# Up-projections of the last layer's experts in four column groups of the array

## The chip, the cores and the metric

The kernel runs on one core of a Trainium2 chip. The metric is the device time of one execution in microseconds. Everything is computed in 32-bit floats. The engines are named as in the profile: PE is TensorE (PEld its weight loads), DVE is VectorE, ACT is ScalarE, POOL is GpSimd, SP issues most transfers.

## The reference, cut to what matters

The input x is 32 batches of 128 tokens with 128 features. Two layers follow each other, each with a residual. The change is in the second, L1:

```python
# L1_cond: two shared experts and eight routed ones, 4096 tokens of 128 features
for e in range(2):
    h = silu(x @ s_w1[e].T) * (x @ s_w3[e].T)      # 128 -> 256
    shared_out += h @ s_w2[e].T                    # 256 -> 128
for e in range(8):
    h = gelu(x @ r_w1[e].T)                        # 128 -> 128
    routed_out += h @ r_w2[e].T * gates_full[:, e] # top 2 of 8
out = (shared_out / 2 + routed_out) / 4
# L1_ffn: a low-rank feed-forward layer on that
P = out @ U1                                       # 128 -> 32
H = gelu(P @ V1 + b1)                              # 32 -> 512
x = x + (H @ U2) @ V2 + b2                         # 512 -> 32 -> 128
```

## The kernel before

Activations are kept with the 128 features on the partitions and the tokens in the free dimension, in 8 blocks of 512 tokens (`TB`). In L1 four blocks make a superblock (`SB = 4`), so there are two superblocks (`NS`). A matmul of one block streams 512 columns and fills one tile of 128 x 512 in PSUM; the pool for these tiles (`mm_tile`) has six buffers, and a second pool (`y_tile`) has two for sums.

The down-projections of the L1 experts are folded with U1 ahead of time (`fold_down`), so that each maps 128 hidden features to 32 outputs. `into` issues four matmuls of 32 columns, one for each block of a superblock: block j writes partitions 32j to 32j+31 of one PSUM tile, which selects column group j of the array. The sum over all experts stays in that tile, `low_p` (`p_ps` in the profile).

The up-projections use the full array. `sh_up` makes, for each of the four blocks, a gate and an up matmul (`g` at line 627, `u` at line 628 of the profile's numbering), then ACT's Silu and DVE's product (`glu`, lines 509 and 510) into `h`. `r_up` makes one matmul per block (`ur`, line 650), ACT's Gelu into `ar` (line 652) and DVE's product with the gate `rg` (line 653), which POOL spreads from one row to all partitions (`spread`, line 504, six buffers). The low-rank layer has its own units: `low_up` (`ul`, line 670) uses four row groups of the array, and its way down (`q_ps`) uses `into` again.

The order is a list of units: the shared ones ("s", 4 for each superblock), the routed ones ("r", 8 for each superblock), and the low-rank ones ("l"). `pipelined` issues the up-projection of unit i+1 ahead of the down-projection of unit i:

```python
units = [("s", sb, k) for sb in range(NS) for k in range(4)]
units += [("r", 0, e) for e in range(E1)]
units += [("r", 1, 0), ("r", 1, 1)]
units += [("l", 0, c) for c in range(NC - 1)]
units += [("r", 1, e) for e in range(2, E1)]
units += [("l", 0, NC - 1)]
units += [("l", 1, c) for c in range(NC)]
```

In between, `l1_scores` (matmuls `l_ps` in column groups, then transposes `l_b` on the full array), `route` and `gates_to_dram` (a transpose `rg_ps`) prepare the second superblock's gates. The framework puts the instructions of each engine in order by their place in the program and by when it expects their inputs, and sets the semaphores. Ahead of L1 lie the L0 layer's experts (up to about 190 us) and its feed-forward part (matmuls `g`, `u` at lines 522 and 523, `yf` at line 209), which ends at 852.3 us.

Of the kernel before, what the change touches and what calls it, by code (L numbers as in the profile page):

```python
# [43 lines left out]
SB = 4  # L44
# [47 lines left out]
def adaln_ffn(  # L92
# [3 lines left out]
    nc = tc.nc  # L96
# [9 lines left out]
    def mm_tile(name):  # L106
        return psum.tile([P, TB], F32, tag="mm", name=name, bufs=6)
# [393 lines left out]
    def spread(row, name):  # L501

        bc = work.tile([P, TB], F32, tag="bc", name=name, bufs=6)
        nc.gpsimd.partition_broadcast(bc, row)  # L504
        return bc

    def glu(ps_gate, ps_up, h, name):
        s = work.tile([P, TB], F32, tag="sg", name=name, bufs=4)
        nc.scalar.activation(s, ps_gate, AF.Silu)  # L509
        V.tensor_tensor(h, s, ps_up, ALU.mult)  # L510
# [76 lines left out]
    sws_t = wpool.tile([P, 2, 2, 2, P], F32, tag="w0", name="sws_t")  # L587
    sw2s_t = wpool.tile([P, 2, 2, P], F32, tag="w1", name="sw2s_t")
    rw1_t = wpool.tile([P, E1, P], F32, tag="w2", name="rw1_t")
# [6 lines left out]
    x1T = xT  # L596
# [19 lines left out]
    def into(y, w, h, first, last):  # L616

        for j in range(SB):
            nc.tensor.matmul(y[32 * j : 32 * (j + 1), :], lhsT=w, rhs=h[:, j, :], start=first, stop=last)  # L619

    def sh_up(sb, k):
        e, c = divmod(k, 2)
        h = work.tile([P, SB, TB], F32, tag="h", name=f"hs_{sb}_{k}", bufs=3)
        for j in range(SB):
            x = x1T[SB * sb + j]
            g, u = mm_tile(f"g1_{sb}_{k}_{j}"), mm_tile(f"u1_{sb}_{k}_{j}")
            nc.tensor.matmul(g, lhsT=sws_t[:, 0, e, c, :], rhs=x, start=True, stop=True)  # L627
            nc.tensor.matmul(u, lhsT=sws_t[:, 1, e, c, :], rhs=x, start=True, stop=True)  # L628
            glu(g, u, h[:, j, :], f"s1_{sb}_{k}_{j}")
        return h  # L630

# [12 lines left out]
    def r_up(sb, e):  # L644
        h = work.tile([P, SB, TB], F32, tag="h", name=f"hr_{sb}_{e}", bufs=3)
        g, k = divmod(e, 4)
        for j in range(SB):
            gate = spread(grows[sb][32 * k : 32 * k + 1, g, j * TB : (j + 1) * TB], f"rg_{sb}_{e}_{j}")
            ps = mm_tile(f"ur_{sb}_{e}_{j}")
            nc.tensor.matmul(ps, lhsT=rw1_t[:, e, :], rhs=x1T[SB * sb + j], start=True, stop=True)  # L650
            a = work.tile([P, TB], F32, tag="sg", name=f"ar_{sb}_{e}_{j}", bufs=4)
            nc.scalar.activation(a, ps, AF.Gelu)  # L652
            V.tensor_tensor(h[:, j, :], a, gate, ALU.mult)  # L653
        return h
# [24 lines left out]
    def low_out(sb):  # L679
        q = work.tile([P, TB], F32, tag="qT", name=f"qT{sb}", bufs=1)  # L680
        V.tensor_copy(q, held["q", sb])
        for j in range(SB):
# [6 lines left out]
            queue.dma_start(out=out[SB * sb + j], in_=t)  # L689

    STAGES = {"s": (sh_up, sh_down), "r": (r_up, r_down), "l": (low_up, low_down)}
    units = [("s", sb, k) for sb in range(NS) for k in range(4)]
    units += [("r", 0, e) for e in range(E1)]
# [112 lines left out]
```

## Time and profile before

| | |
|---|---|
| median of 3 runs | 1026.9 us (1026.76 to 1027.1) |
| the profiled execution's own time | 1027.21 us |
| its span, first to last instruction | 1025.4 us |
| mean granted TensorE clock | 0.998 |
| TensorE busy | 1010.3 us, 99% of the span, 2894 matmul records |
| shared and routed part of L1 | 852.3 to 1000.2 us |
| what follows (last low-rank units, output) | 1000.2 to 1025.4 us |

An fp32 matmul appears as two records and two weight loads. Matmuls overlap in the pipeline, so the busy time and the duration of a record are longer than what it adds; the distance between starts tells what a matmul costs. In a line of the timeline the first number is the start in us, the second the length of the stretch, "x8" the records merged into it; "128\*32" are the rows and columns of the array that a matmul uses. What stands in brackets is idle time ahead and what ended it.

### The profile page before, as it was taken

What the parts mean: (1) busy time and instruction counts of PE and PEld (TensorE: products, weight loads), DVE (VectorE), ACT (ScalarE), POOL (GpSimd) and SP (SyncE); (2) the same over time, 40 slices, a digit from 0 to 9 for tenths busy, and PEclk for the clock granted to TensorE, in tenths of its full rate; (3) what the DMA queues carried; (4) which work ended last, traced back from release to release, by engine and by line L of the source; (5) the groups of instructions that cost most, each with busy time, mean ns of one, the idle gap of its engine ahead of it and who ended that gap; (6) DMA issues with size and microseconds to landing.
All of it is one profiled execution on the core that took longest, in us unless ns stands there. A gap on an engine that the chain in (4) does not pass through costs nothing.

```text
span 1025.4 us, 8650 instructions
## 1 busy us (share of the span) xinstructions
PE 1010.3 (99%) x2894; PEld 484.4 (47%) x2894; DVE 457.3 (45%) x811; ACT 332.8 (32%) x575; POOL 143.9 (14%) x142
## 2 busy tenths in 40 slices
PE   7999999999999999999999999999999999999997
PEld 3378888444445444444444444444444444333332
DVE  4424443445433434343436444444433334547582
ACT  4445444423221222222223222222222223335754
POOL 0000000031111111111111111111111002008670
PEclk9999999999999999999999999999999999999999
DMA  9235555000000000000000000000000000000002
GB/s 316 94 125 165 176 169 167 25 2 1 3 2 0 1 0 2 0 1 1 1 0 1 0 3 2 0 1 0 1 0 1 0 1 3 1 5 1 1 1 82
DMA packets 18699, 34.66 MB, mean 34 GB/s; under 512 B 1680, under 2 KB 9872, under 8 KB 18640
## 3 DMA queue, kind: packets, MB, share of 16 engines
q1 hardware_dynamic: 17792, 32.61, 9.9%
q10 hardware_dynamic: 864, 1.52, 0.4%
q8 instruction: 22, 0.36, 0.1%
q14 instruction: 21, 0.17, 0.1%
HBM read 31.76 MB, written 2.36 MB: 33 GB/s over the span
## 4 chain that ended last, share of the span: by engine, by line
PE 98%; DVE 1%; DMA 0%; DVEq 0%; issue 0%; ACTq 0%
PE yf L209 21%; PE g L522 21%; PE u L523 21%; PE y L209 6%; PE u L203 6%; PE ur L650 6%; PE us L203 3%; PE g L627 3%; PE u L628 3%; PE p_ps L619 2%; PE ys L209 2%; PE ul L670 1%; PE q_ps L619 1%; DMA sw_t<-in_sw 0%; PE fold_ps L603 0%; PE o_ps L685 0%
## 5 line engine op out<-in xcount | busy, mean ns | idle before, releaser
L509 ACT ACTIVATE sf<-g 128x512 f32<-128x512 f32 x256 | 152.7, 597 | 495.4 <-PE g L522 494.3
L510 DVE TENSOR_TENSOR hf<-sf,u 128x512 f32<-128x512 f32 x256 | 175.8, 687 | 207.2 <-PE u L523 206.1
L522 PE MATMUL g<-c0all,wg_t 128*128 128x512 f32 x512 | 261.6, 592 | 0.0
L523 PE MATMUL u<-c0all,wu_t 128*128 128x512 f32 x512 | 261.4, 592 | 0.0
L209 PE MATMUL yf<-hf,wd_t 128*128 128x512 f32 x512 | 230.5, 592 | 0.0
L504 POOL PARTITION_BROADCAST fg<-fgT x64 | 77.8, 1228 | 720.2 <-DVE tf L536 516.5
L209 PEld LDWEIGHTS yf<-hf,wd_t 128*128 128x128 f32 x512 | 97.0, 190 | 123.0 <-issue 123.0
L523 PEld LDWEIGHTS u<-c0all,wu_t 128*128 128x128 f32 x512 | 97.3, 190 | 122.4 <-issue 120.5
L522 PEld LDWEIGHTS g<-c0all,wg_t 128*128 128x128 f32 x512 | 96.7, 190 | 120.5 <-issue 118.4
L536 DVE TENSOR_TENSOR tf<-yf,fg 128x512 f32<-128x512 f32 x64 | 44.2, 691 | 167.5 <-PE yf L209 162.0
L504 POOL PARTITION_BROADCAST rg<-grows x64 | 65.0, 1118 | 129.9 <-DVE hr L653 80.3
L204 ACT ACTIVATE h<-u,w 128x256 f32<-128x256 f32 x136 | 58.5, 474 | 62.1 <-PE u L203 62.1
L653 DVE TENSOR_TENSOR hr<-ar,rg 128x512 f32<-128x512 f32 x64 | 56.6, 911 | 24.4 <-ACT ar L652 22.9
L203 PE MATMUL u<-x,w 128*128 128x256 f32 x272 | 64.3, 379 | 0.0
L209 PE MATMUL y<-h,w 128*128 128x256 f32 x272 | 64.3, 379 | 0.0
L650 PE MATMUL ur<-xall,rw_t 128*128 128x512 f32 x128 | 59.2, 605 | 0.0
L203 PEld LDWEIGHTS u<-x,w 128*128 128x128 f32 x272 | 51.7, 190 | 7.9 <-issue 1.0
L209 PEld LDWEIGHTS y<-h,w 128*128 128x128 f32 x272 | 51.7, 190 | 7.5 <-issue 0.5
L652 ACT ACTIVATE ar<-ur 128x512 f32<-128x512 f32 x64 | 37.9, 598 | 32.8 <-PE ur L650 31.1
L537 DVE TENSOR_TENSOR xall<-xall,tf 128x512 f32<-128x512 f32 x64 | 45.4, 709 | 2.1
L650 PEld LDWEIGHTS ur<-xall,rw_t 128*128 128x128 f32 x128 | 23.0, 189 | 36.4 <-issue 25.2
L388 DVE SCALAR_TENSOR_TENSOR t<-y,w 128x256 f32<-128x256 f32 x34 | 16.5, 484 | 53.0 <-PE y L209 53.0
(168 smaller groups left out, 472.9 us busy)
## 6 DMA issues: line engine op xcount, KB each, us to landing
w<-in_experts SPq DMA_DIRECT2D x34, 578.5 KB
xall<-in_x SPq DMA_DIRECT2D x8, 256.0 KB
wg_t<-in_w_gate SPq DMA_DIRECT2D x8, 256.0 KB
wu_t<-in_w_up SPq DMA_DIRECT2D x8, 256.0 KB
wd_t<-in_w_down SPq DMA_DIRECT2D x8, 256.0 KB
rw_t<-in_r_w SPq DMA_DIRECT2D x2, 512.0 KB
out<-fin SPq DMA_DIRECT2D x4, 256.0 KB
out<-fin ACTq DMA_DIRECT2D x4, 256.0 KB
```

The costliest lines, as they stand in the source:

```text
L203: nc.tensor.matmul(ps[c], lhsT=w[:, c * P : (c + 1) * P], rhs=rhs, start=True, stop=True)
L204: nc.scalar.activation(h[:, c, :], ps[c], AF.Gelu_apprx_tanh, bias=bias[:, c : c + 1])
L209: nc.tensor.matmul(y[:, :n], lhsT=w[:, c, :], rhs=h[:, c, :n], start=(c == 0), stop=(c == NC - 1))
L504: nc.gpsimd.partition_broadcast(bc, row)
L509: nc.scalar.activation(s, ps_gate, AF.Silu)
L510: V.tensor_tensor(h, s, ps_up, ALU.mult)
L522: nc.tensor.matmul(g, lhsT=wg_t[:, e, cs], rhs=c0T[blk], start=True, stop=True)
L523: nc.tensor.matmul(u, lhsT=wu_t[:, e, cs], rhs=c0T[blk], start=True, stop=True)
L536: V.tensor_tensor(t, y, spread(fgates[blk][32 * k : 32 * k + 1, g, :], f"fg_{blk}_{e}"), ALU.mult)
L537: V.tensor_tensor(xT[blk], xT[blk], t, ALU.add)
L650: nc.tensor.matmul(ps, lhsT=rw1_t[:, e, :], rhs=x1T[SB * sb + j], start=True, stop=True)
L653: V.tensor_tensor(h[:, j, :], a, gate, ALU.mult)
```

## The change

A helper `from_x` issues an up-projection as four matmuls, each with 32 of the 128 weight columns and with the same x. Matmul j writes partitions 32j to 32j+31 of the same PSUM tile, that is, it uses column group j. `sh_up` and `r_up` call it in place of their full matmuls. What is computed, the tiles and the readers stay the same.

```diff
+    def from_x(ps, w, x):
+
+        for j in range(4):
+            own = slice(32 * j, 32 * (j + 1))
+            nc.tensor.matmul(ps[own, :], lhsT=w[:, own], rhs=x, start=True, stop=True)
+
     def sh_up(sb, k):
...
-            nc.tensor.matmul(g, lhsT=sws_t[:, 0, e, c, :], rhs=x, start=True, stop=True)
-            nc.tensor.matmul(u, lhsT=sws_t[:, 1, e, c, :], rhs=x, start=True, stop=True)
+            from_x(g, sws_t[:, 0, e, c, :], x)
+            from_x(u, sws_t[:, 1, e, c, :], x)
...
     def r_up(sb, e):
...
-            nc.tensor.matmul(ps, lhsT=rw1_t[:, e, :], rhs=x1T[SB * sb + j], start=True, stop=True)
+            from_x(ps, rw1_t[:, e, :], x1T[SB * sb + j])
```

## The prediction, made before the changed kernel ran

> **What bounds the kernel now.** I read the page's busy times first, then the chain of waits, then the timeline of the stretch that the change edits, and last the windows of the three parts of that stretch.
>
> ```profile
> PE 1010.3 (99%) x2894; PEld 484.4 (47%) x2894; DVE 457.3 (45%) x811; ACT 332.8 (32%) x575; POOL 143.9 (14%) x142
> ...
> PE 98%; DVE 1%; DMA 0%; DVEq 0%; issue 0%; ACTq 0%
> ```
>
> TensorE is busy for 99% of the span and carries 98% of the chain that ended last. What counts is how many matmul passes TensorE streams and what it loses between them. An fp32 matmul leaves two records (two passes). The shared up-projections show the price of a pass:
>
> ```profile
> 888.94 1.02 PE L627 MATMUL g<-xall,sws_t 128*128 128x512 f32 x2
> 889.80 1.02 PE L628 MATMUL u<-xall,sws_t 128*128 128x512 f32 x2
> 890.66 1.02 PE L627 MATMUL g<-xall,sws_t 128*128 128x512 f32 x2
> 891.51 1.02 PE L628 MATMUL u<-xall,sws_t 128*128 128x512 f32 x2
> 892.47 1.06 PE L619 MATMUL p_ps<-hs,fold 128*32 128x512 f32 x8
> 893.46 1.12 PE L627 MATMUL g<-xall,sws_t 128*128 128x512 f32 x2
> ```
>
> The reader is to read starts, not durations, since the records overlap. Full matmuls start 0.858 us apart (888.94 to 891.51 is three of them, 2.57), so a pass costs 0.429. The down-projection is one row of eight records: four matmuls of 32 columns, two passes each, and the next full matmul starts 0.99 after it. Four quarter-wide matmuls together thus cost little more than one full one. But the seams are not free: 891.51 to 892.47 is 0.96 where 0.858 would do, and 892.47 to 893.46 is 0.99. The routed stage repeats this, and shows the other engines:
>
> ```profile
> 922.33 3.70 PE L650 MATMUL ur<-xall,rw_t 128*128 128x512 f32 x8
> ...
> 925.96 1.07 PE L619 MATMUL p_ps<-hr,fold 128*32 128x512 f32 x8
> ...
> 926.96 3.70 PE L650 MATMUL ur<-xall,rw_t 128*128 128x512 f32 x8
> ...
> 929.73 4.11 POOL L504 PARTITION_BROADCAST rg<-grows  x4 [0.49 <-DVE hr L653]
> ...
> 931.58 0.30 PEld L650 LDWEIGHTS ur<-xall,rw_t 128*128 128x128 f32 x2 [0.84 <-ACT ar L652]
> ```
>
> A routed unit takes 4.63 us (922.33 to 926.96, and 4.627 as the mean to 936.21). It streams 8 passes up and 2 down: 10 x 0.4292 = 4.292. So 0.335 is lost per unit in going from the full array to four column groups and back. A shared unit takes 8.06 (884.41 to 892.47) for 18 passes, 7.725: again 0.335. By single starts, going into column groups loses 0.117 (0.094 before the first, 0.024 before the second pass, whose weights were not loaded ahead), going back 0.218. The two weight loads bunched at 931.58, "x2" in 0.30, are the back side of it: they could not be loaded ahead.
>
> What happens between two column-group sets, with no full matmul between:
>
> ```profile
> 866.16 1.07 PE L619 MATMUL p_ps<-hs,fold 128*32 128x512 f32 x8
> ...
> 867.04 1.04 PE L421 MATMUL l_ps<-xall,par 128*32 128x512 f32 x8
> ...
> 867.90 1.02 PE L619 MATMUL p_ps<-hs,fold 128*32 128x512 f32 x2
> ```
>
> 866.16, 867.04, 867.90: 0.88, then 0.86. Nothing is lost between sets of one shape, though weights, sources and targets all change.
>
> **The change part by part.** Each of 128 full matmuls (64 shared: 8 units x 4 blocks x gate and up; 64 routed: 16 x 4) becomes four of 32 columns, side by side, into the four partition quarters of the same tile.
>
> *Streaming.* A set of four streams 512 columns per group, twice, as the full matmul did: 0.858 by the rows above. Cost against before: zero, if four streams run at once. Here the four read one x, where the down-projection reads four slices; no row shows that. The streams start some 7 ns apart, so they are not on one address at one time. I take zero; the other end, two streams at a time, would be 128 x 0.86 = +110 us, and nothing in the trace points there.
>
> At this place the Trainium skill speaks against the change: "TensorE: Matmul & The Clock Gate", section Measured speedup vs the span model, gives four row groups 3.07 times and three column groups 2.38 times one matmul's rate, not 4 and 3. At 77% of the ideal a set would cost 0.858 / 0.77 = 1.11, and 128 sets +33 us. This case's row (0.88 and 0.86 per set of four) is 97 to 100%. I take the row: those figures look like ones for a lone set with its latency, but here sets follow one another.
>
> *Seams removed.* Counted along TensorE's order from 852.33 to 1000.20. Into column groups: 7 in the shared part, 10 up to 962.98, 6 after 970.90, together 23. Back to the full array: 5 in the shared part (that ahead of rg_ps stays), 9, then 1 at 970.90 and 5 after, together 20. New ones into column groups: 3, where the first shared up follows yf (852.33), and after the transposes l_b and rg_ps. Net 20 in and 20 back, 20 x 0.335 = 6.7 us. The seams of the low-rank units (ul in row groups) and of the transposes stay. All 20 lie on the chain, where TensorE never idles (the windows show it busy 65.40 of 65.40 and 82.50 of 82.50 us).
>
> *Instructions added.* 128 x 3 x 2 = 768 weight loads and as many matmul records. A set of four is 8 pairs of load and matmul in 0.858 us, one pair per 107 ns. Is that rate to be had for long? Bounds from the trace: at 63 to 150 us TensorE runs 405 pairs in 87 us with no gap, 215 ns a pair, but streaming sets that pace. fold_ps has 24 pairs 112 ns apart, set by their 128-column loads. Five tiny matmuls (gate_ps to t_ps, 10 pairs) take 31 ns a pair, and from 962.98 to 970.90 there are 56 pairs at 141 ns, every hole of which has a named waiter. All short ones can come from a filled queue, so the trace bounds the sustained cost of a pair only between 31 and 215 ns. The same page (Part 1, Wait — 56ns, not 53.3ns?) gives 62 ns of sequencer work per MATMUL if hardware decode is off: 8 x 62 = 0.50 per set, hidden under 0.858; if a load cost as much, 0.99 per set and not hidden. Its section Back-to-back issue gap gives 81 ns for a load-matmul pair in a stream: 0.65, hidden. I take zero, the nearest rows being the bursts, and keep the dear end as a rival. Instruction fetch: the page's 22 packets (0.36 MB) grow by about a quarter, with DMA at 1% in this stretch; the stage at 63 to 150 us uses up instructions at half the needed rate without a stall. Zero.
>
> *Waits.* Each set signals about 20 ns later (the last of four). ACT and DVE start later by that, TensorE does not. In the shared part ACT idles 1.12 us before each activation, so it follows; its idle time covers the 4% faster pace.
>
> *What is late next.* In the routed part a unit shrinks to 4.29. POOL needs 4.11 for its four broadcasts; DVE 3.5 for four products. Both slow each other when both are full:
>
> ```profile
> 974.20 10.91 DVE L653 TENSOR_TENSOR hr<-ar,rg 128x512 f32<-128x512 f32 x11 [9.30 <-ACT ar L652]
> ...
> 974.98 10.79 POOL L504 PARTITION_BROADCAST rg<-grows  x10 [8.75 <-DVE hr L653]
> ```
>
> That is 0.99 a product and 1.08 a broadcast, against 1.073 per block from TensorE. DVE keeps up; POOL is level with it, and starts six tiles ahead (six buffers). Cost zero, with little room. The tail from 1000.20 (25.2 us, paced by ACT, DVE and the output) only moves earlier.
>
> **Sum.** 0 (streaming) + 0 (issue) + 0 (waits) - 6.7 = -6.7 us. The profiled execution took 1027.2 (span 1025.4), so it would be 1020.5; it stands 0.3 above the median of the runs, 1026.9, and the median becomes 1020.2.
>
> **The rivals.**
>
> *Issue cannot keep four groups fed* (slower). Place: the 152 sets, 128 up and 24 down, between 852 and 1000. It decides above 107 ns for a pair of load and matmul; at 113 ns it eats the whole gain (152 x 8 x 5.5 ns = 6.7). With 62 ns for a load as for a matmul, 124 a pair, it is 152 x 0.133 = +20.2, less 6.7: 1040.4. For: no row shows a pair under 112 ns for longer than a queue may hold, and the routed and shared stages need it for 55 us and more. Against: the small bursts at 31 ns, and the 81 ns of the page. Chance 0.16.
>
> *POOL or DVE sets the pace of the routed part* (a smaller gain). The page's mean of a routed broadcast is 1118 ns: 4.47 per unit, 0.18 over 4.29, over 16 units 2.9 us, less the lead of six tiles that hides some. With waits handed back and forth it may be 4: 1021 to 1024. Chance 0.09. For: 0.49 of POOL's time per unit is a wait for DVE. Against: the saturated stretch at 974.20, where it ran 1.08.
>
> *The seams stay or come back in another form* (no change): for instance weights of a column group that are exposed at each set, 0.05 x 128 = 6.4. The l_ps row speaks against it. 1026.5 to 1027, chance 0.05.
>
> **How the numbers follow.** Full gain 0.70, 1020.2, within 1018.5 (a TensorE hole such as the 0.1 us ahead of l_b filled, one seam more or less) and 1021.5. Adding the second rival and the lower part of the third gives 8 in 10 up to 1025. The runs of this kernel lie within 0.03%, and about 0.2%, 2 us, is what a measurement can tell from no change. Faster by over 0.2%: 0.70 + 0.08 = 0.78; same: 0.05 + 0.01 = 0.06; slower: 0.16.
>
> **What would show it.** Right: the page counts 3662 matmul records; in the timeline the routed unit takes 4.29 and the shared one 7.73; up and down rows of 128*32 follow each other with no 0.52 between last starts; p_ps ends about 6.7 us earlier, near 993.5; the tail is unchanged. Issue bound: sets of four start 0.95 to 1.0 apart with no releaser named but "issue", evenly. POOL bound: TensorE gaps only in the routed part, ahead of p_ps, released by DVE hr, DVE waiting for rg. The prediction is wrong if four groups reading one x stream slower than 0.86 per set, or if the order of matmuls comes out differently and lets p_ps split the sets.

## The result, and the profile after

The changed kernel takes 1020.67 us (median of 6 runs, 1020.39 to 1021.55), the kernel before 1027.07 beside it: 6.4 us less, a ratio of 0.9938 with a 95% interval of 0.9926 to 0.9951. Forecast were 1020.2 us, 6.7 us less. The profiled execution took 1021.55 us, with a span of 1019.6.

The page of the kernel after, first the busy times, then the chain:

```profile
PE 1004.8 (99%) x3662; PEld 478.4 (47%) x3662; DVE 460.4 (45%) x811; ACT 332.6 (33%) x575; POOL 145.7 (14%) x142
...
PE 98%; DVE 1%; DMA 0%; DVEq 0%; issue 0%; ACTq 0%
```

TensorE has 768 records and as many weight loads more, is still busy for 99%, and still carries 98% of the chain. The time came out of TensorE itself. The timeline of TensorE in the shared part of the kernel after:

```profile
914.49 1.04 PE L625 MATMUL g<-xall,sws_t 128*32 128x512 f32 x8
915.35 1.04 PE L625 MATMUL u<-xall,sws_t 128*32 128x512 f32 x8
916.20 1.04 PE L619 MATMUL p_ps<-hs,fold 128*32 128x512 f32 x8
917.06 1.47 PE L625 MATMUL ur<-xall,rw_t 128*32 128x512 f32 x12
```

and in the routed part:

```profile
921.35 3.62 PE L625 MATMUL ur<-xall,rw_t 128*32 128x512 f32 x32
924.79 1.04 PE L619 MATMUL p_ps<-hr,fold 128*32 128x512 f32 x8
925.65 3.62 PE L625 MATMUL ur<-xall,rw_t 128*32 128x512 f32 x32
929.08 1.04 PE L619 MATMUL p_ps<-hr,fold 128*32 128x512 f32 x8
929.94 2.33 PE L625 MATMUL ur<-xall,rw_t 128*32 128x512 f32 x20
```

Every row starts a whole number of 0.858 us after the one ahead: 914.49, 915.35, 916.20, 917.06, and 921.35 to 924.79 is four of them. The 0.96 and 0.99 around the down-projection are gone. A routed unit takes 4.29 us (921.35, 925.65, 929.94) where it took 4.63.

All starts of the part, from the first shared matmul to the last down-projection, can be added up. Each full matmul of 512 columns, or set of four, is charged 0.858, a single quarter of a set a quarter of that, a transpose of 128 columns 0.107; what is left between starts is loss. The part of it that stands at a change of tile shape is what the prediction calls a seam:

| from the first shared matmul to the last p_ps | before | after |
|---|---|---|
| whole, us | 147.87 | 141.19 |
| streaming as charged, up to the last start, us | 137.49 | 137.49 |
| loss between shared, routed and down matmuls | 6.72 | 0.08 |
| loss around l_b and rg_ps | 1.07 | 1.41 |
| loss around ul and q_ps | 2.60 | 2.21 |

Streaming is a charge here and not a measurement: that it is the same says only that as many columns stream. That a set of four takes no longer than a full matmul is shown by the starts above, and by the 0.08 us that are left between sets. The loss fell from 10.39 to 3.70 us: 6.68 less, with the rounding.

### The profile page after: what moved, and what is told of

Its sections match the earlier page's. It is cut to its first block, busy times and chain, and to the rows that moved or that the text cites. A ratio compares the mean times of both kernels' runs of the same rounds, so it can differ in the third digit from the quotient of the medians.

```text
span 1019.6 us, 10200 instructions
## 1 busy us (share of the span) xinstructions
PE 1004.8 (99%) x3662; PEld 478.4 (47%) x3662; DVE 460.4 (45%) x811; ACT 332.6 (33%) x575; POOL 145.7 (14%) x142
## 4 chain that ended last, share of the span: by engine, by line
PE 98%; DVE 1%; DMA 0%; DVEq 0%; issue 0%; ACTq 0%
PE yf L209 22%; PE g L522 22%; PE u L523 22%; PE u L203 6%; PE y L209 6%; PE ur L625 5%; PE us L203 3%; PE g L625 3%; PE u L625 3%; PE ys L209 2%; PE p_ps L619 2%; PE ul L676 1%; PE q_ps L619 1%; DMA sw_t<-in_sw 0%; PE fold_ps L603 0%; PE o_ps L691 0%
## 5 line engine op out<-in xcount | busy, mean ns | idle before, releaser
L659 DVE TENSOR_TENSOR hr<-ar,rg 128x512 f32<-128x512 f32 x64 | 59.9, 981 | 15.9 <-ACT ar L658 15.4
L625 PE MATMUL ur<-xall,rw_t 128*32 128x512 f32 x512 | 58.4, 592 | 0.0
L625 PE MATMUL g<-xall,sws_t 128*32 128x512 f32 x256 | 42.0, 593 | 0.0
L625 PE MATMUL u<-xall,sws_t 128*32 128x512 f32 x256 | 42.0, 592 | 0.0
```

Source lines behind the costliest of these rows:

```text
L625: nc.tensor.matmul(ps[own, :], lhsT=w[:, own], rhs=x, start=True, stop=True)
```

## The experiments

Times of whole kernels carry some tenths from elsewhere in the program, so each verdict rests on two numbers: the timed runs, and the length of this part in the profile. The one repeat of that second number, the changed kernel run again beside e9, gave 141.20 after 141.19.

**One half of the change alone.** In e1 `r_up` keeps its full matmul (the edit below, against the changed kernel), in e2 `sh_up` does.

```diff
-            from_x(ps, rw1_t[:, e, :], x1T[SB * sb + j])
+            nc.tensor.matmul(ps, lhsT=rw1_t[:, e, :], rhs=x1T[SB * sb + j], start=True, stop=True)
```

Expected of e1:

> Only the shared up-projections are issued in column groups; the routed ones keep the full array. Theory (the gain is the seams removed, 0.117 us into column groups and 0.218 us back): of the shared part's seams 7 into column groups go and 3 new ones come, and 4 back go (the one ahead of the first routed unit stays): 4 x 0.117 + 4 x 0.218 = 1.3 us faster than before. Rival (four quarter-wide matmuls stream faster or slower than a full one, so the effect goes with the number of matmuls): half of the 6.4 us, 3.2, since 64 of the 128 matmuls are shared.

Expected of e2:

> Only the routed up-projections are issued in column groups. Theory (seams): 16 seams into column groups and 16 back go and none comes, 16 x 0.335 = 5.4 us faster than before. Rival (effect per matmul): 3.2 us, as for the shared half.

Measured: e1 1025.92 beside 1027.27 us, ratio 0.9986 (0.9979 to 0.9992), this part 146.44, so 1.43 shorter than before. e2 1022.14 beside 1027.27, ratio 0.9946 (0.9933 to 0.9960), this part 142.62, 5.25 shorter. The rows of TensorE show the seams that each keeps, first the routed ones of e1, then the shared ones of e2:

```profile
921.63 3.70 PE L656 MATMUL ur<-xall,rw_t 128*128 128x512 f32 x8
925.26 1.06 PE L619 MATMUL p_ps<-hr,fold 128*32 128x512 f32 x8
926.26 3.70 PE L656 MATMUL ur<-xall,rw_t 128*128 128x512 f32 x8
```

```profile
892.27 1.02 PE L634 MATMUL u<-xall,sws_t 128*128 128x512 f32 x2
893.22 1.07 PE L619 MATMUL p_ps<-hs,fold 128*32 128x512 f32 x8
894.21 1.13 PE L633 MATMUL g<-xall,sws_t 128*128 128x512 f32 x2
```

Both halves have 64 matmuls, yet one brings nearly four times the other. The effect goes with the number of seams, not of matmuls. 1.43 and 5.25 add up to 6.68. In e1, as in the changed kernel, the new seam of 0.09 between `yf` and the first shared matmul lies ahead of this part and is not in these numbers (last section).

**Fewer seams without column groups.** e3 takes the kernel before and issues two units at a time (its tile buffers change too, as the expectation says):

```diff
...
+    while at < len(units):
+        n = 1 if units[at][0] == "l" else 2
+        groups.append(units[at : at + n])
+        at += n
...
+    pipelined(groups, group_up, group_down)
```

> The kernel before, with full up-projections, but shared and routed units taken in pairs: two up-projections, then the two down-projections of the pair before. Four buffers for h in place of three, and two small tiles share others' buffers to make room. Theory (seams): about half of the seams go, 13 instead of 23 into column groups and 10 instead of 20 back, 10 x 0.335 = 3.3 us faster than before, some tenths more or less from the changed order around the low-rank units. Rival (the gain comes from column groups as such, their loads or their streaming): no change.

Measured: 1024.99 beside 1027.27 us, ratio 0.9980 (0.9972 to 0.9987); this part 145.90, so 1.97 shorter, where 3.3 was expected. The loss between shared, routed and down matmuls fell from 6.72 to 3.18, 3.54 less: the seams did go, with full matmuls only. The way into the low-rank units took 1.6 of it back. The timeline of e3, TensorE, shows the place:

```profile
959.43 2.76 PE L620 MATMUL p_ps<-hr,fold 128*32 128x512 f32 x18
962.93 1.14 PE L671 MATMUL ul<-pT,par 32*128 32x512 f32 x8 [0.73 <-DVE pT L662]
```

With both down-projections of a pair issued together, the low-rank up-projection comes straight behind the sum it reads, and waits for DVE's copy of it. In the kernel before a routed up-projection stood between.

**Is it the full array, or any change of shape?** e4 uses two groups of 64 columns:

```diff
-        for j in range(4):
-            own = slice(32 * j, 32 * (j + 1))
+        for j in range(2):
+            own = slice(64 * j, 64 * (j + 1))
```

> The changed kernel with two groups of 64 columns in place of four of 32. Theory that a seam is paid for any change of tile shape: the seams between 64 and 32 columns stay and some new ones come at the edges, so about the time of before (1026.5 to 1027.5). Rival, that a seam is paid only between the whole array and column groups: about the time of the changed kernel (1020 to 1021). Two groups of 64 should stream at the same 0.858 us per set.

Measured: 1026.76 beside 1027.27 us, ratio 0.9995 (0.9987 to 1.0004); this part 147.29, 0.58 shorter. The timed runs cannot tell it from no change. The timeline of e4, TensorE:

```profile
923.50 3.65 PE L625 MATMUL ur<-xall,rw_t 128*64 128x512 f32 x16
927.08 1.07 PE L619 MATMUL p_ps<-hr,fold 128*32 128x512 f32 x8
928.08 2.37 PE L625 MATMUL ur<-xall,rw_t 128*64 128x512 f32 x10
```

923.50 to 928.08 is 4.58: the unit still loses 0.29 of 0.335, and from the down-projection to the next matmul it is 1.00 as before. So two groups of 64 stream at full rate too, but a seam is paid between these two shapes as well. What the change needs is not smaller tiles but the same tiles as its neighbour.

The weight loads show what became cheaper, first the kernel before, then e4:

```profile
926.96 0.30 PEld L650 LDWEIGHTS ur<-xall,rw_t 128*128 128x128 f32 x2 [0.84 <-ACT ar L652]
927.49 0.19 PEld L650 LDWEIGHTS ur<-xall,rw_t 128*128 128x128 f32 x1 [0.24 <-issue]
```

```profile
928.07 0.20 PEld L625 LDWEIGHTS ur<-xall,rw_t 128*64 128x64 f32 x4 [0.84 <-ACT ar L658]
928.56 0.14 PEld L625 LDWEIGHTS ur<-xall,rw_t 128*64 128x64 f32 x2 [0.29 <-issue]
```

The third load of a unit (in e4, of each group) starts with its second pass. The second pass comes 0.53 us after the first in the kernel before and 0.48 in e4 (by the starts in ns), where 0.43 would do: the second load behind a seam, not made ahead, costs 0.10 with 128 columns and 0.05 with 64. The rest of the seam, 0.10 ahead of `p_ps` and 0.11 behind it in e4, is about what it was (0.09 and 0.11). What TensorE does in that time no run shows.

**How much issue is there to spare?** e5 and e6 cut each matmul along the tokens, into two and four:

```diff
+        n = TB // 4
+        for i in range(4):
+            t = slice(i * n, (i + 1) * n)
...
-            nc.tensor.matmul(ps[own, :], lhsT=w[:, own], rhs=x, start=True, stop=True)
+                nc.tensor.matmul(ps[own, t], lhsT=w[:, own], rhs=x[:, t], start=True, stop=True)
```

Expected of e5:

> The changed kernel with each matmul of the up-projections cut in two along the tokens (256 columns streamed instead of 512): twice as many pairs of weight load and matmul for the same streaming, one pair per 54 ns where the changed kernel needs one per 107. Theory (issue has room): the time of the changed kernel, 1020.7, up to 1.5 us more for the extra starts. Rival (issue is near its limit): with c ns a pair a set costs 16 c once that is over 858; at c = 62 it is 0.99 us and the kernel 128 x 0.134 = 17 us slower than the changed one.

Expected of e6:

> As the one with half rows, but cut in four (128 columns streamed): one pair per 27 ns. Here the limit should show: at 31 ns a pair (the burst of tiny matmuls ahead of the gates) a set of 32 pairs costs 0.99 us and the kernel is 17 us slower than the changed one; at 62 ns 1.98 us and 144 us slower; if nothing limits at 27 ns, within 3 us of the changed one. The time gives c.

Measured: e5 1021.14 us, this part 141.80; e6 1022.34 us, this part 143.02. Both stay close to the changed kernel: 0.61 and 1.83 us longer in this part, which is 4.8 ns for each of the 128 and 384 added sets (two passes each, so 2.4 ns a pass). The timeline of e6, TensorE:

```profile
921.53 3.68 PE L628 MATMUL ur<-xall,rw_t 128*32 128x128 f32 x128
925.03 1.04 PE L619 MATMUL p_ps<-hr,fold 128*32 128x512 f32 x8
```

128 pairs of load and matmul in 3.50 us (921.53 to 925.03) are 27 ns a pair. The changed kernel needs one per 107. Between units come the eight pairs of a down-projection at 107 ns, during which later pairs might be made ready; over a whole routed unit, 136 pairs in 4.35 us, it is 32 ns. That rate was held through the routed units without a limit showing. Whether 27 ns could be held without these breaks was not tried.

**Does POOL or DVE pace the routed part?** e7 spreads one gate row per unit:

```diff
-            gate = spread(grows[sb][32 * k : 32 * k + 1, g, j * TB : (j + 1) * TB], f"rg_{sb}_{e}_{j}")
+            if j == 0:
+                gate = spread(grows[sb][32 * k : 32 * k + 1, g, :TB], f"rg_{sb}_{e}")
```

> The changed kernel, with one gate row spread for each routed unit in place of four, used for all its blocks (the gates of three blocks in four are left out): POOL does a quarter of its work there and DVE is no longer slowed by it. Theory (TensorE alone paces the routed part after the change): the time of the changed kernel within 0.5 us. Rival (POOL or DVE paces it, or holds the last sum back): 1 to 4 us faster.

Measured: 1020.27 us, this part 141.10 (0.09 shorter), what follows it 24.88 in place of 25.19. That 0.31 came behind the issue of the last output transfers (1014.78 us, in e7 1014.48: 20.35 behind the last p_ps in both), where POOL and DVE have no work left. So over this part POOL and DVE cost TensorE 0.09. At one place they did hold it: in the changed kernel a quarter of the down-projection behind the first low-rank unit waits for DVE's last product, in e7 none does (changed kernel first, then e7):

```profile
961.16 1.43 PE L619 MATMUL p_ps<-hr,fold 128*32 128x512 f32 x8
961.55 0.14 PEld L619 LDWEIGHTS p_ps<-hr,fold 128*32 128x32 f32 x2 [0.23 <-DVE hr L659]
```

```profile
960.95 1.07 PE L619 MATMUL p_ps<-hr,fold 128*32 128x512 f32 x8
```

By the count of the table above, e7 gains 0.36 there and loses 0.28 of it again between `ul` and `q_ps`. The timelines of DVE and POOL in the changed kernel show how near it is later on:

```profile
970.42 23.10 DVE L659 TENSOR_TENSOR hr<-ar,rg 128x512 f32<-128x512 f32 x24 [8.93 <-ACT ar L658]
...
971.20 19.33 POOL L504 PARTITION_BROADCAST rg<-grows  x18 [8.38 <-DVE hr L659]
```

DVE makes the last 24 products in one go, 0.963 each, without a pause, while TensorE delivers one per 1.073; POOL needs 1.074. DVE comes late out of the low-rank units and works off its arrears just in time: it ends at 993.5, and the last down-projection starts at 993.95. In e7 the same products take 0.6 to 0.75 each and DVE waits for ACT:

```profile
977.08 1.48 DVE L660 TENSOR_TENSOR hr<-ar,rg 128x512 f32<-128x512 f32 x2 [1.09 <-ACT ar L659]
978.73 0.69 DVE L660 TENSOR_TENSOR hr<-ar,rg 128x512 f32<-128x512 f32 x1 [0.17 <-ACT ar L659]
```

**The seams of the transposes.** e8 makes l_b and rg_ps of the second superblock in column groups, as matmuls with the identity (shown for rg_ps):

```diff
...
+        for j in range(4 if (kind, sb) == ("r", 1) else 0):
+            own = slice(32 * j, 32 * (j + 1))
+            nc.tensor.matmul(ps[own, :P], lhsT=flat[:, own], rhs=ident, start=True, stop=True)
```

> The changed kernel, with the two transposes that lie within this part (scores and gates of the second superblock) made in four column groups too, as matmuls with the identity. Theory (seams): one seam back and one into column groups at the gates' transpose go, and one into column groups behind the scores' transposes; the way into those is covered by a wait for DVE. 0.335 + 0.117 = 0.45 us faster than the changed kernel, at the edge of what can be told. Rival (transposes pay less for a seam, being short): no change.

Measured: 1021.12 us, this part 141.29: no gain. The loss between matmuls did fall, from 3.70 to 3.27 us, 0.44 as expected, but streaming, charged as above, rose by 0.54. The two timelines of TensorE, first the changed kernel, then e8:

```profile
869.71 0.66 PE L436 MATMUL l_b<-ident,l1T 128*128 128x128 f32 x4
870.29 1.06 PE L625 MATMUL g<-xall,sws_t 128*32 128x512 f32 x8
```

```profile
869.48 1.08 PE L441 MATMUL l_b<-ident,l1T 128*32 128x128 f32 x32
870.38 1.04 PE L638 MATMUL g<-xall,sws_t 128*32 128x512 f32 x8
```

A transpose is one pass (4 records for four), a matmul with the identity is two (32 records for sixteen quarters). l_b to the next matmul is 0.58 in the one and 0.90 in the other. The seam saved was dearer to buy than to pay.

**One more wait taken out.** Of the 3.70 us of loss that are left (3.3 in the expectation below, which charged the last set in full), 0.78 lie ahead of l_b, where TensorE waits for a copy on DVE and one quarter of a down-projection alone runs meanwhile (weight loads, changed kernel):

```profile
869.70 0.42 PEld L436 LDWEIGHTS l_b<-ident,l1T 128*128 128x128 f32 x4 [0.88 <-DVE l1T L423]
```

e9 issues the scores of the second superblock one unit earlier:

```diff
+        if (sb, k) == (0, 1):
+            logits_ahead("l1", par[:, AT["r1x"]], xT, 1)
```

Expected of e9, and of the changed kernel run again beside it:

> The changed kernel, with the score matmuls of the second superblock (l_ps) issued ahead of the second shared up-projection, so that DVE's copy of them is done when TensorE reaches the transposes l_b. Theory: of the 3.3 us that the changed part still loses between its matmuls, 0.78 lie ahead of l_b, 0.58 of that a wait for this copy; that goes, and the rest (seam into and out of the transposes) stays: 0.5 to 0.65 us less than the changed kernel within this part, about 1020.1, at the edge of what the timed runs can tell. Rival (the order of the other instructions shifts and opens another hole): no change.

> The changed kernel itself, on the same chip as the one with the scores ahead: 1020.7, and 141.2 us from the first shared matmul to the last down-projection, if the time of this part doesn't vary from run to run.

Measured: e9 1020.02 us, the changed kernel 1020.42 on the same chip; this part 140.32 against 141.20. In the profile that is 0.88 less, more than the 0.5 to 0.65 expected: 0.67 of it ahead of l_b, and another 0.2 at rg_ps, which the expectation did not have. In the timed runs the 0.4 us between them cannot be told from nothing. The timeline of e9, TensorE:

```profile
867.20 1.04 PE L619 MATMUL p_ps<-hs,fold 128*32 128x512 f32 x8
868.17 0.66 PE L436 MATMUL l_b<-ident,l1T 128*128 128x128 f32 x4
868.76 1.07 PE L625 MATMUL g<-xall,sws_t 128*32 128x512 f32 x8
```

867.20 to 868.17 is 0.97: a set and its seam, and no wait. Against the kernel before, e9 has a ratio of 0.9929 (0.9915 to 0.9942).

## Why the prediction was right

- *Streaming at no cost*: right. Sets of four that read the same x start 0.858 us apart, as full matmuls did. By the prediction's estimate, the 77% of the ideal that it took from the Trainium skill (TensorE: Matmul & The Clock Gate, Measured speedup vs the span model) would have made this part 33 us longer; sets that follow one another do not pay that here.
- *Seams, 20 pairs of 0.335*: right, 6.7 expected; measured 6.68 in this part, less the 0.09 of the new seam ahead of it, 6.59. e1 and e2 have the split that the count gives (1.3 and 5.4 expected; 1.43 less the same 0.09, and 5.25 measured), and e3 removes seams without column groups. e4 narrows the cause: it is the change of shape that costs. That the sum comes within 0.1 is partly luck, since single waits moved both ways by more (see Waits).
- *Issue*: right, and now measured. The 124 ns a pair at which the prediction worked out its slower rival is nearly four times the 32 ns that e6 held.
- *Waits*: put at zero, and near that in sum, but not one by one. The set in front of rg_ps and the low-rank units kept their seams, and single entries moved by some tenths: the loss ahead of ul rose from 0.41 to 0.81, with DVE's late product of e7's section, and that between ul and q_ps fell from 0.98 to 0.73.
- *POOL and DVE*: right that TensorE stays the bound, but nearer than the text had it. It took the rates alone; the sign that it names for this rival, a gap ahead of p_ps released by DVE, came once (961.55; DVE did not wait for POOL there), and DVE's arrears from the low-rank units left 0.4 us ahead of the last sum.
- *Tail*: 25.19 us after 25.21, unchanged. The last p_ps came at 994.43, not 993.5: this part began 0.90 later, at 853.23, for a reason outside of the change (last section). That is why the profiled span fell by only 5.8.

## What to carry to other kernels

On a kernel that TensorE paces, look at starts around each change of tile shape, not at busy time: 99% busy hid 6.7 us. Where short tiled matmuls alternate with full ones, give the full ones the tiling of their neighbours; four column groups with one moving operand streamed like one full matmul here (fp32, 512 columns, set behind set). Before removing the next seam, compare its price with what the substitute streams, as the transposes showed.

## What was not expected of the hardware

TensorE's granted clock is not the same in two profiled executions. In the kernel before, the window from 46 to 51 us has a granted clock of 1.00, in the changed one 0.66 (the column behind POOL's; first the kernel before):

```profile
46.00:51.00 5.00, 5.00 (x13) 2.12 (x13) 2.01 (x13) 2.75 (x4) 0.00 (x0) 1.00 0.50 169
```

```profile
46.00:51.00 5.00, 5.00 (x9) 1.92 (x8) 1.15 (x8) 2.23 (x4) 0.00 (x0) 0.66 0.66 237
```

The code there is the same. In the changed kernel's execution five intervals between passes, from 46.36 to 50.20 us, are 0.62 to 0.86 us long in place of 0.43, and cost 1.69 us together. In the first 11 us it had been 0.88 ahead, so the part of the change begins 0.81 later by this, and 0.09 by its new first seam: the first shared matmul starts 0.52 us behind the last `yf` pass, where it was 0.43. The slow stretch does not belong to the changed kernel: its second profiled execution (e10) has 1.00 in this window. Six of the twelve profiled executions have 0.66 (the changed kernel's first, e2, e4, e5, e7, e8). In both kernels TensorE has just waited 1.97 us for DVE there; why only some executions are throttled was not tried.

Column groups can also be at different matmuls. In both kernels one quarter of a down-projection runs ahead of l_b. Full matmuls follow in the kernel before; in the changed one, one group is then a matmul further than the other three for the following units (TensorE, changed kernel):

```profile
884.91 0.59 PE L625 MATMUL g<-xall,sws_t 128*32 128x512 f32 x1
884.91 0.60 PE L619 MATMUL p_ps<-hs,fold 128*32 128x512 f32 x3
```

Three groups stream p_ps while the fourth is at the next g. They come together again at the transpose rg_ps, where the loss was 0.32 us and is 0.12 in e9, in which no group is ahead. The trace gives starts and not the order of issue, so whether one group overtook the others in the array or was put ahead of them in the queue is not shown.
